# A graph layer with a Winograd-style convolution: the filter transform moved from VectorE to TensorE products

## The chip, the cores and the metric

The kernel runs on one core of one Trainium2 chip. The metric is the device time of one execution in microseconds. Engines are named as in the profile: PE is the matrix engine (PEld its weight loads), DVE the vector engine, ACT the scalar engine, POOL the GpSimd engine, SP the engine that issues most DMAs. Every engine executes its own instructions in the order in which the program lists them; a DMA is issued by SP, ACT or POOL and stands in that engine's order too.

## The reference

The input is x of 64 graphs with 256 nodes and 256 channels, and a 0/1 adjacency of 64 x 256 x 256. All is float32. After a layer norm and a rectifier (h), each graph goes through this layer, whose result is added to x:

```python
xc = jnp.transpose(x, (0, 2, 1))
h = jax.nn.relu(_bn(_conv1d(xc, conv1_w, 0), ...))           # 256 -> 256, one tap
h = _bn(_conv1d(h, conv2_w, 8), ...)                         # 256 -> 256, 17 taps along the nodes
x_conv = jnp.transpose(jax.nn.relu(h + xc), (0, 2, 1))
s = x @ w_se.T + b_se                                        # 3 numbers a node
A = jnp.exp(-dist(s)) * mask
x_nmp = A @ jax.nn.relu(x @ w_msg.T + b_msg)
gi = concat([x_conv, x_nmp]) @ w_ih.T + b_ih                 # then a GRU cell with
gh = x @ w_hh.T + b_hh                                       # gates r, z, n
```

The convolution with 17 taps (conv2) is the heavy part. It is computed in a transformed domain: along the nodes the signal is cut into pieces of 16, and a product of two polynomials is found from their values at 15 complex and 2 real points, arranged as 16 "bins": bins 0 to 14 are the complex points (roots of unity of several orders) and need three real products each, and bin 15 holds the two points 1 and -1 with one product each. So 15 x 3 + 2 = 47 matrices of 256 x 256 are needed from the filter. They are the filter's values at those points: the real part, and two combinations of real and imaginary part. The filter has 256 x 256 channel pairs with 17 taps each.

## The kernel before

**Units.** Two graphs form a pair (G = 2), handled as a tile of 512 columns (W); four pairs form a batch (PB = 4), and there are 8 batches (NB). conv2 works on a batch at a time, the other parts on a pair.

**The start.** The program first loads x for two pairs (SP), the taps of conv2 for the first 128 input channels (ACT, 17 DMAs), weights, and on POOL the small vectors (`vec`, line 375) and the adjacency. Lines 427 to 462 then transform the filter. Input channels lie on partitions. For each half of them (k = 0, 1) ACT copies the taps (line 433), DVE runs the same odd and even transforms that are used for the data (class `Fft`, `odd` at line 67 and `even` at line 97; their instructions have lines 55, 58 and 61), and `put` (line 425) stores each result from SP to `filt` in DRAM. `filt` is laid out by bin, then partition, kind of product, half and output channel, so that one bin is a block of 768 KB, 6 KB for each partition. The same buffers U, V, PT, Sv, T serve the filter here and the data later. Then come w_ih and w_hh (loaded by ACT), the batch norm vectors of conv2, and the sums of biases (`b_rz` at line 471, on DVE).

**Preparation of a pair.** `norm` (line 512) takes statistics of x on DVE, a power on POOL (line 526) and scales on DVE (line 530). `transpose_h` (line 534) transposes on PE, rectifies on ACT into HT, and issues the load of x two pairs ahead. `conv1` (line 548) does the one-tap convolution on PE and writes h1 from ACT (line 555). `split` (line 560) forms the sums and differences of h1 in U and V on DVE (lines 569 and 570). Before the first batch the four pairs are prepared one after the other (lines 779 to 783). Later preparations are spread between the gates of the batch before.

**The data's transform.** `forward` (line 771) queues the odd and even transforms of the batch on a list. The class `Pace` decides at each DVE instruction of the main order how many list entries to emit before it: it keeps estimated clocks of PE and DVE and emits entries as long as DVE is estimated to have time. `pace.flush(mark)` emits the rest up to a mark. `products` needs the odd part.

**The batch.** `products(b, m)` (line 596) does the bins 2m and 2m + 1 on PE, with weights from three rotating tiles WB. `load_bin` (line 575) loads bin n from `filt` on SP; the load of a bin waits until the tile's former bin has been used. Between the products stand `embed` (line 642), `message` (line 652), `affinity` (line 666), `transpose_a`, `aggregate`; after them the back transform, the residual and the `gates` (line 704). All PE products carry line 500 in the profile, all transposes line 504, since two helpers record them. A float32 product appears as two MATMUL records. PSUM has five tiles "acc" and three tiles "aux" of 512 columns. `load_y` (line 353) loads x again for the final addition, from POOL, the first two before the first preparation.

Of the kernel before, what the change touches and what calls it, by code (L numbers as in the profile page):

```python
# [3 lines left out]

# [34 lines left out]
class Fft:  # L39
# [221 lines left out]


class Mark:
    left = False
# [6 lines left out]
def kernel(  # L271
# [26 lines left out]
    nc = tc.nc  # L298
# [18 lines left out]
    const = ctx.enter_context(tc.tile_pool(name="const", bufs=1))  # L317
    work = ctx.enter_context(tc.tile_pool(name="work", bufs=1))
    psum = ctx.enter_context(tc.tile_pool(name="psum", bufs=1, space=bass.MemoryType.PSUM))
    dram = ctx.enter_context(tc.tile_pool(name="dram", bufs=1, space=bass.MemoryType.DRAM))  # L320
# [32 lines left out]
    def load_y(i):  # L353
        Y[i] = work.tile([P, G * MC, D], FP, name="y", bufs=2)
        load_rows(Y[i], x, i, nc.gpsimd)
# [6 lines left out]
    SL = GB * DC * L * NW  # L362
    Ut, Vt, Yvt = (const.tile([P, SL], FP, name=n) for n in ("U", "V", "Yv"))
    PTt, Svt, Tt = (const.tile([P, SL // 2], FP, name=n) for n in ("PT", "Sv", "T"))
# [27 lines left out]

    def load_taps(k):
        V = Slots(Vt, 1, L // 2, D)
        taps = c2_wT[k * P:(k + 1) * P]
        for c in range(2):
            for s in range(L // 2):
                t = L - (2 * (s - 4) + c) if s >= 4 else L - (8 + 2 * s + c)
                nc.scalar.dma_start(out=V(c, s)[:, 0, 0, :], in_=taps[:, t, :])
        w0 = work.tile([P, W], FP, name="tr")  # L400
        nc.scalar.dma_start(out=w0[:, :D], in_=taps[:, 0, :])
        return w0

    w0 = load_taps(0)
    w_c1 = const.tile([P, DC, D], FP)
    nc.sync.dma_start(out=w_c1, in_=c1_wT.rearrange("(k p) o -> p k o", p=P))
    w_se = const.tile([P, DC, KD], FP)
    nc.vector.memset(w_se, 0.0)
# [5 lines left out]
    s1, h1_shift = fold_bn(bn1, "bn1")  # L414
    w_msg = const.tile([P, DC, D], FP)
# [4 lines left out]


    filt = dram.tile([BINS, P, 3, DC, D], FP, name="filt")

    def put(bins, kind, k, t):
        nc.sync.dma_start(out=filt[bins:bins + t.shape[1], :, kind, k, :].rearrange("n p o -> p n o"), in_=t)

    for k in range(DC):
        if k > 0:
            w0 = load_taps(k)
        U, V = (Slots(t, 1, L // 2, D) for t in (Ut, Vt))  # L430
        PT, Sv, T = (Slots(t, 1, L // 4, D) for t in (PTt, Svt, Tt))
        for c in range(2):
            nc.scalar.copy(U(c, 0, 8), V(c, 0, 8))
        e0 = w0[:, :D].rearrange("p (a n e) -> p a n e", a=1, n=1)
        nc.vector.tensor_add(U(0, 4), V(0, 4), e0)
        nc.vector.tensor_sub(V(0, 4), V(0, 4), e0)
        for _, step in fft.odd(V, T, Sv):
            step()
        for c in range(2):
            put(c * 4, 0, k, V(c, 4, 4)[:, 0])  # L440
            put(c * 4, 2, k, Sv(c, 0, 4)[:, 0])
        nc.vector.tensor_sub(V(None, 0, 4), V(None, 0, 4), V(None, 4, 4))
        for c in range(2):
            put(c * 4, 1, k, V(c, 0, 4)[:, 0])
        for _, step in fft.even(U, PT, T):
            step()
        for c in range(2):
            put(8 + c * 2, 0, k, U(c, 0, 2)[:, 0])
            put(8 + c * 2, 2, k, U(c, 4, 2)[:, 0])
            put(12 + c, 0, k, PT(c, 2)[:, 0])  # L450
            put(12 + c, 2, k, U(c, 6)[:, 0])
        put(14, 0, k, PT(0, 1)[:, 0])
        put(14, 2, k, U(0, 7)[:, 0])
        put(15, 0, k, U(1, 7)[:, 0])
        put(15, 1, k, PT(1, 0)[:, 0])
        nc.vector.tensor_sub(U(None, 2, 2), U(None, 2, 2), U(None, 0, 2))
        nc.vector.tensor_sub(PT(None, 3), PT(None, 3), PT(None, 2))
        nc.vector.tensor_sub(PT(1, 1), PT(1, 1), PT(0, 1))
        for c in range(2):
            put(8 + c * 2, 1, k, U(c, 2, 2)[:, 0])  # L460
            put(12 + c, 1, k, PT(c, 3)[:, 0])
        put(14, 1, k, PT(1, 1)[:, 0])

    w_ih = const.tile([P, 2 * DC, 3 * D], FP)
    nc.scalar.dma_start(out=w_ih, in_=ih_wT.rearrange("(k p) o -> p k o", p=P))
    w_hh = const.tile([P, DC, 3 * D], FP)
    nc.scalar.dma_start(out=w_hh, in_=hh_wT.rearrange("(k p) o -> p k o", p=P))
    s2, h2_shift = fold_bn(bn2, "bn2", 1.0 / L)
# [17 lines left out]

    U, V, Yv = (Slots(t, GB * DC, L // 2, NW) for t in (Ut, Vt, Yvt))
    PT, Sv, T = (Slots(t, GB * DC, L // 4, NW) for t in (PTt, Svt, Tt))
# [5 lines left out]
    def acc():  # L494
        return psum.tile([P, W], FP, name="acc", bufs=5)
# [3 lines left out]
    def mm(p, w, v, columns, **kw):  # L499
        nc.tensor.matmul(p, w, v, **kw)  # L500
        pace.tensor(columns)
# [69 lines left out]


    WB = {}

    def load_bin(b, n):
        b, n = b + n // BINS, n % BINS
        if b < NB:
            WB[b, n] = work.tile([P, 3, DC, D], FP, name="wb", bufs=3)
            kinds = 3 if n < BINS - 1 else 2
            nc.sync.dma_start(out=WB[b, n][:, :kinds], in_=filt[n, :, :kinds])  # L580

# [14 lines left out]
    def products(b, m):  # L596
        load_bin(b, 2 * m + 2)
        p = [acc() for _ in range(3)]
        for n in range(2):
            for kind, v in enumerate(operands(2 * m + n)):  # L600
                if v is None:
                    continue
                for o in range(DC):
                    for k in range(DC):
                        mm(p[kind][:, (n * DC + o) * P:(n * DC + o + 1) * P],
                           WB[b, 2 * m + n][:, kind, k, o * P:(o + 1) * P],
                           v[:, k::DC, 0, :], P, start=(k == 0), stop=(k == DC - 1))
# [73 lines left out]
    def transpose_a(i):  # L681
        AT[i] = work.tile([P, G, MC, N], FP, name="aT")
        for g in range(G):
            q = aux()
            for c in range(MC):
                for r in range(MC):
                    transpose(q[:, c * N + r * P:c * N + (r + 1) * P], E[i][:, g, r, c * P:(c + 1) * P])
            nc.scalar.copy(AT[i][:, g].rearrange("p c n -> p (c n)"), q)  # L688

    def aggregate(i):  # L690
        XNM[i] = work.tile([P, DC, W], FP, name="xnm", bufs=2)
# [12 lines left out]
    def gates(i, dc, wait=None):  # L704
# [10 lines left out]
        product(ghn, h, n, True, True)  # L715
        gn = work.tile([P, W], FP, name="gn", bufs=2)
        nc.scalar.activation(gn, ghn, AF.Identity, bias=b_hh[:, 2 * DC + dc:2 * DC + dc + 1])
# [6 lines left out]
        product(pr, xc, r, False, True)  # L724
        tr = work.tile([P, W], FP, name="tr")
        nc.scalar.activation(tr, pr, AF.Tanh, bias=b_rz[:, dc:dc + 1], scale=0.5)  # L726
# [4 lines left out]
        nc.vector.scalar_tensor_tensor(gn, gn, 0.5, pn, op0=ALU.mult, op1=ALU.add)  # L731
        nn = work.tile([P, W], FP, name="nn", bufs=2)
        nc.scalar.activation(nn, gn, AF.Tanh, bias=b_ih[:, 2 * DC + dc:2 * DC + dc + 1])
        product(pz, xc, z, False, True)
        tz = work.tile([P, W], FP, name="tz")
# [3 lines left out]
        d = OT[i, dc] = work.tile([P, W], FP, name="d", bufs=3)  # L739
        nc.vector.tensor_sub(d, HT[i][:, dc, :], nn)  # L740
# [30 lines left out]
    def forward():  # L771
        pace.add(fft.odd(V, T, Sv), odd)
        pace.add(fft.even(U, PT, T), even)

    load_bin(0, 0)
    load_bin(0, 1)
    load_y(0)
    load_y(1)
    for j in range(PB):
        norm(j)  # L780
        transpose_h(j)
        conv1(j)
        split(j)
    forward()
    for b in range(NB):
# [120 lines left out]
```

## Time and profile before

| what | value |
|---|---|
| time, median of 3 runs | 2196.8 us (2194.21 to 2197.34) |
| profiled execution, its time | 2198.26 us |
| its span on the core | 2196.5 us |
| busy: PE, DVE, ACT, POOL | 1904.0, 1497.1, 623.5, 170.3 us |
| mean granted PE clock | 0.969 |
| DMA | 186.95 MB, mean 85 GB/s |

The profile is one execution, taken by the hardware profiler. Busy times are sums over an engine's instructions. In the rows of the time line, the number in front is the start in microseconds from the start of the span, the second the length of the row, then engine, line, operation, result and sources, and in brackets how long the engine stood idle before it and what ended the wait. "SPq" and the like are the DMA issues of an engine. In the busy tenths, each digit is a slice of 55 us. A share of the DMA engines of 1.00 means that all 16 are busy.

### The profile page before, as it was taken

Reading aid. Unit: us, or ns where it says so; the run is one execution under the profiler, and the core shown is the slowest. Engines: PE = TensorE matmul, PEld = TensorE weight load, DVE = VectorE, ACT = ScalarE, POOL = GpSimd, SP = SyncE. Lnnn points to the kernel's source line nnn. Section 1 sums busy time; section 2 is a strip of 40 time slices with the busy share of each in tenths; the row PEclk is TensorE's granted clock in tenths of the full one; section 3 lists DMA queues with packets and bytes.
Section 4 is the critical chain, followed back from the end, with each engine's and each line's share of the span. In section 5 each row is a group of like instructions: output and inputs, shape, how many; then the busy total and the mean of one; then the engine's idle time right before and its main releaser. Section 6 shows DMA issues by size and latency. Waiting matters only on the chain.

```text
span 2196.5 us, 20806 instructions
## 1 busy us (share of the span) xinstructions
PE 1904.0 (87%) x7744; PEld 1189.0 (54%) x7744; DVE 1497.1 (68%) x2737; ACT 623.5 (28%) x997; POOL 170.3 (8%) x255
## 2 busy tenths in 40 slices
PE   0023989999899989999899989999899989999897
PEld 0012944568444954568444854568445864468453
DVE  5866993678738784588738695587738785597622
ACT  0011243224232243224322243223322243222321
POOL 2010000010000000100000000100010000100000
PEclk9996999999999999999999999999999999999999
DMA  4551611245012620235012520326012530225011
GB/s 128 177 152 33 200 50 31 62 126 161 11 42 60 202 67 27 65 110 169 19 39 63 185 84 20 72 77 202 19 39 53 184 95 24 48 63 178 10 29 29
DMA packets 74453, 186.95 MB, mean 85 GB/s; under 512 B 19792, under 2 KB 36688, under 8 KB 74352
## 3 DMA queue, kind: packets, MB, share of 16 engines
q1 hardware_dynamic: 40448, 128.20, 17.8%
q0 software_dynamic: 28208, 50.60, 10.5%
q10 hardware_dynamic: 5696, 6.82, 1.0%
q8 instruction: 61, 1.00, 0.2%
q14 instruction: 40, 0.33, 0.0%
HBM read 156.39 MB, written 29.10 MB: 84 GB/s over the span
## 4 chain that ended last, share of the span: by engine, by line
PE 74%; DVE 14%; DMA 3%; ACT 2%; issue 2%; POOL 1%; POOLq 0%; DVEq 0%; ACTq 0%
PE acc L500 56%; PE aux L500 15%; PE aux L504 3%; DMA wb<-filt 3%; DVE V L55 2%; DVE V L58 2%; DVE T L61 1%; DVE T L58 1%; DVE Yv L61 1%; DVE V L61 1%; DVE Yv L638 1%; DVE e L677 1%; ACT Yv L639 1%; DVE T L55 1%; POOL rstd L526 0%
## 5 line engine op out<-in xcount | busy, mean ns | idle before, releaser
L500 PE MATMUL acc<-Yv,w_ih 128*128 128x512 f32 x768 | 357.4, 617 | 46.8 <-ACT Yv L639 46.8
L500 PE MATMUL acc<-hT,w_hh 128*128 128x512 f32 x768 | 350.6, 592 | 0.0
L500 PE MATMUL acc<-xnm,w_ih 128*128 128x512 f32 x768 | 350.4, 592 | 0.0
L500 PEld LDWEIGHTS acc<-Yv,w_ih 128*128 128x128 f32 x768 | 151.6, 199 | 243.4 <-issue 185.8
L500 PEld LDWEIGHTS acc<-xnm,w_ih 128*128 128x128 f32 x768 | 145.9, 190 | 183.7 <-issue 183.7
L500 PEld LDWEIGHTS acc<-hT,w_hh 128*128 128x128 f32 x768 | 144.1, 190 | 161.6 <-issue 156.4
L726 ACT ACTIVATE tr<-acc,b_rz 128x512 f32<-128x512 f32 x64 | 44.0, 687 | 553.6 <-PE acc L500 553.6
L504 PE MATMUL aux<-ident,x 128*128 128x128 f32 x256 | 40.3, 299 | 182.5 <-DVE x L530 161.3
L728 DVE SCALAR_TENSOR_TENSOR gn<-tr,gn 128x512 f32<-128x512 f32 x64 | 44.2, 691 | 209.3 <-ACT tr L726 209.3
L55 DVE SCALAR_TENSOR_TENSOR V<-T,V 128x256 f32<-128x256 f32 (+2 forms) x280 | 149.8, 609 | 0.5
L569 DVE TENSOR_TENSOR V<-h 128x512 f32<-128x512 f32 x64 | 44.0, 688 | 145.9 <-ACT h L555 145.9
L504 PEld LDWEIGHTS aux<-ident,x 128*128 128x128 f32 x256 | 32.0, 150 | 196.8 <-DVE x L530 163.8
L500 PE MATMUL acc<-V,wb 128*128 128x128 f32 x1024 | 128.9, 281 | 0.0
L500 PE MATMUL aux<-w_msg,hT 128*128 128x256 f32 x512 | 116.5, 380 | 12.9 <-ACT rd L649 12.9
L500 PE MATMUL aux<-aT,msg 128*128 128x256 f32 x512 | 126.0, 403 | 0.6 <-ACT aT L688 0.6
L500 PEld LDWEIGHTS acc<-V,wb 128*128 128x128 f32 x1024 | 124.0, 198 | 0.0
L500 PEld LDWEIGHTS acc<-U,wb 128*128 128x128 f32 x1024 | 120.0, 192 | 5.1 <-issue 2.5
L500 PE MATMUL acc<-U,wb 128*128 128x128 f32 x1024 | 122.1, 275 | 0.0
L500 PE MATMUL acc<-hT,w_c 128*128 128x512 f32 x256 | 119.3, 610 | 0.0
L500 PEld LDWEIGHTS aux<-w_msg,hT 128*128 128x128 f32 x512 | 96.1, 190 | 35.2 <-ACT rd L649 14.6
L500 PEld LDWEIGHTS aux<-aT,msg 128*128 128x128 f32 x512 | 102.3, 204 | 19.5 <-issue 3.8
L500 PE MATMUL acc<-Sv,wb 128*128 128x128 f32 x512 | 71.4, 285 | 37.8 <-DVE Sv L58 25.2
(134 smaller groups left out, 2640.1 us busy)
## 6 DMA issues: line engine op xcount, KB each, us to landing
wb<-filt SPq DMA_DIRECT2D x120, 768.0 KB
x<-in_x_dram SPq DMA_DIRECT2D x64, 256.0 KB
adj<-in_adj_dram POOLq DMA_DIRECT2D x64, 256.0 KB, 6.1
y<-in_x_dram POOLq DMA_DIRECT2D x64, 256.0 KB, 5.5
out_dram<-y POOLq DMA_DIRECT2D x64, 256.0 KB, 5.2
V<-in_c_wT_dram ACTq DMA_DIRECT2D x32, 128.0 KB
filt<-V SPq DMA_DIRECT2D x8, 512.0 KB
wb<-filt SPq DMA_DIRECT2D x8, 512.0 KB
```

The source lines that it names most:

```text
L55: return self.step(out, lambda: self.v.scalar_tensor_tensor(out, x, s, y, op0=ALU.mult, op1=ALU.add))
L58: return self.step(out, lambda: self.v.tensor_add(out, x, y))
L61: return self.step(out, lambda: self.v.tensor_sub(out, x, y))
L500: nc.tensor.matmul(p, w, v, **kw)
L504: nc.tensor.transpose(p, v, ident)
L569: nc.vector.tensor_sub(V(None, s, 4)[:, A], a, bb)
L638: nc.vector.scalar_tensor_tensor(v, v, s2[:, o:o + 1], HT[i][:, o, :], op0=ALU.mult, op1=ALU.add)
L639: nc.scalar.activation(v, v, AF.Relu, bias=h2_shift[:, o:o + 1])
L677: nc.vector.tensor_mul(e, e, ADJ[i][:, g * MC + c].rearrange("p (b h c) -> p c h b", c=MC, b=NW))
L726: nc.scalar.activation(tr, pr, AF.Tanh, bias=b_rz[:, dc:dc + 1], scale=0.5)
L728: nc.vector.scalar_tensor_tensor(gn, tr, 1.0, gn, op0=ALU.add, op1=ALU.mult)
```

## The change

Values of a polynomial with 17 coefficients at given points are a product with a constant matrix. The change forms that matrix (`filter_points`) for three groups of bins, 0 to 5, 6 to 11 and 12 to 15, with 18, 18 and 11 columns (kinds), and does the product on PE. Seven input channels with 17 taps each are laid on 119 partitions; the constant matrix is block-diagonal, 119 x 126 (or 119 x 77), so one product of 256 columns gives 7 channels x 18 kinds (or 11) on partitions, with the 256 output channels along the free dimension. Each half of 128 channels makes 18 such groups; the 2 + 2 channels left over form one more tile of 68 rows. A step `filters(m, j)` takes two groups: two products into one "acc" tile, one ACT copy into a staging tile ("fo", six of them), one store from SP. Three groups of bins x 19 steps are 57 steps. The first 48 stand in the preparation loop, twelve after each pair's `split`; nine stand after `forward`.

What else is moved:

- `norm(0)` stands before the loop, and `norm(j + 1)` between `transpose_h(j)` and `conv1(j)`.
- `filt` is three DRAM tiles (one for each group of bins), each by half, partition, kind, output channel. `load_bin` therefore fetches, for each partition, two pieces of up to 3 KB instead of one of up to 6 KB, and WB's inner order is half, kind.
- The first two `load_bin`, then w_ih and w_hh (now on SP), stand after the second pair's steps. The two `load_y` stand after all steps.
- The small vectors (`vec`) are loaded by SP instead of POOL, the weights of conv1 by ACT instead of SP, and the zeroing of w_se is on POOL instead of DVE.
- The taps, the constant matrices and the staging tiles live in a pool "stage" that is closed after the steps; its memory is used again by a pool "late" that holds Yv, y and the tiles of the gates.

```diff
+def filter_points(bins, taps):
+    cols = []
+    for n in bins:
+        z = [(ROOTS[n] if n < 15 else 1.0) ** (taps - 1 - t) for t in range(taps)]
+        if n < 15:
+            cols += [[v.real for v in z], [v.imag - v.real for v in z], [v.real + v.imag for v in z]]
+        else:
+            cols += [[1.0] * taps, [(-1.0) ** (taps - 1 - t) for t in range(taps)]]
+    return np.array(cols, np.float64).T
...
-        nc.gpsimd.dma_start(out=t, in_=src.rearrange("(k p) -> p k", p=P))
+        nc.sync.dma_start(out=t, in_=src.rearrange("(k p) -> p k", p=P))
...
-    def load_taps(k):
-        V = Slots(Vt, 1, L // 2, D)
...
+    KG = P // TAPS
+    NG = P // KG
+    REST = P - NG * KG
+    taps = stage.tile([KG * TAPS, DC * NG + 1, D], FP, name="taps")
+
+    def load_taps(dc, a, b, eng):
+        eng.dma_start(out=taps[:, dc * NG + a:dc * NG + b, :],
+                      in_=c2_wT[dc * P + a * KG:dc * P + b * KG].rearrange("(g k) t o -> (k t) g o", k=KG))
+
     w_c1 = const.tile([P, DC, D], FP)
-    nc.sync.dma_start(out=w_c1, in_=c1_wT.rearrange("(k p) o -> p k o", p=P))
+    nc.scalar.dma_start(out=w_c1, in_=c1_wT.rearrange("(k p) o -> p k o", p=P))
+    s1, h1_shift = fold_bn(bn1, "bn1")
+    PASSES = [range(0, 6), range(6, 12), range(12, 16)]
+    points = []
+    for n, bins in enumerate(PASSES):
+        f = filter_points(bins, TAPS)
+        m = np.zeros((KG, TAPS, KG, f.shape[1]), np.float32)
+        for k in range(KG):
+            m[k, :, k] = f
+        t = stage.tile([KG * TAPS, KG * f.shape[1]], FP, name=f"points{n}")
+        nc.scalar.dma_start(out=t, in_=nc.inline_tensor(m.reshape(KG * TAPS, -1), name=f"points{n}").ap())
+        points.append(t)
+    for dc in range(DC):
+        for h in range(2):
+            load_taps(dc, h * NG // 2, (h + 1) * NG // 2, nc.scalar if dc else nc.sync)
+        nc.sync.dma_start(out=taps[dc * REST * TAPS:(dc + 1) * REST * TAPS, DC * NG, :],
+                          in_=c2_wT[dc * P + NG * KG:(dc + 1) * P].rearrange("k t o -> (k t) o"))
...
-    for k in range(DC):
-        if k > 0:
-            w0 = load_taps(k)
...
-        for _, step in fft.odd(V, T, Sv):
-            step()
...
+    filt = [dram.tile([DC, P, t.shape[1] // KG, D], FP, name=f"filt{n}") for n, t in enumerate(points)]
+
+    def filters(m, j):
+        kinds = filt[m].shape[2]
+        groups = range(2 * j, min(2 * j + 2, DC * NG + 1))
+        size = REST * DC if groups[0] == DC * NG else KG
+        p = acc()
+        for n, g in enumerate(groups):
+            mm(p[:size * kinds, n * D:(n + 1) * D], points[m][:size * TAPS, :size * kinds],
+               taps[:size * TAPS, g, :], D, start=True, stop=True)
+        t = stage.tile([P, 2, D], FP, name="fo", bufs=6)
+        nc.scalar.copy(t[:size * kinds, :len(groups)].rearrange("p n o -> p (n o)"),
+                       p[:size * kinds, :len(groups) * D])
+        if size == KG:
+            dc, g = divmod(groups[0], NG)
+            nc.sync.dma_start(out=filt[m][dc, g * KG:(g + 2) * KG].rearrange("(g k) t o -> (k t) g o", k=KG),
+                              in_=t[:size * kinds])
...
-            WB[b, n] = work.tile([P, 3, DC, D], FP, name="wb", bufs=3)
...
-            nc.sync.dma_start(out=WB[b, n][:, :kinds], in_=filt[n, :, :kinds])
+            WB[b, n] = work.tile([P, DC, 3, D], FP, name="wb", bufs=3)
+            kinds, m = 3 if n < BINS - 1 else 2, n // len(PASSES[0])
+            first = 3 * (n - PASSES[m][0])
+            nc.sync.dma_start(out=WB[b, n][:, :, :kinds, :].rearrange("p k t o -> p k (t o)"),
+                              in_=filt[m][:, :, first:first + kinds, :].rearrange("k p t o -> p k (t o)"))
...
-    load_bin(0, 0)
-    load_bin(0, 1)
+    steps = [(m, j) for m in range(len(PASSES)) for j in range(NG + 1)]
+    norm(0)
+    for j in range(PB):
+        transpose_h(j)
+        norm(j + 1) if j + 1 < PB else None
+        conv1(j)
+        split(j)
+        for m, n in steps[j * 12:(j + 1) * 12]:
+            filters(m, n)
+        if j == 1:
+            load_bin(0, 0)
+            load_bin(0, 1)
+            nc.sync.dma_start(out=w_ih, in_=ih_wT.rearrange("(k p) o -> p k o", p=P))
+            nc.sync.dma_start(out=w_hh, in_=hh_wT.rearrange("(k p) o -> p k o", p=P))
+    forward()
+    for m, n in steps[PB * 12:]:
+        filters(m, n)
+    stage_ctx.close()
+    late = ctx.enter_context(tc.tile_pool(name="late", bufs=1, reuse_waits="tile"))
+    Yvt = late.tile([P, SL], FP, name="Yv")
+    Yv = Slots(Yvt, GB * DC, L // 2, NW)
     load_y(0)
     load_y(1)
-    for j in range(PB):
-        norm(j)
-        transpose_h(j)
-        conv1(j)
-        split(j)
-    forward()
```

More of the change, by code (lines that the diff above doesn't have):

```diff
@@ L318 @@
     work = ctx.enter_context(tc.tile_pool(name="work", bufs=1))
+    stage_ctx = ExitStack()
+    stage = stage_ctx.enter_context(tc.tile_pool(name="stage", bufs=1))
     psum = ctx.enter_context(tc.tile_pool(name="psum", bufs=1, space=bass.MemoryType.PSUM))
@@ L353, in load_y @@
     def load_y(i):
-        Y[i] = work.tile([P, G * MC, D], FP, name="y", bufs=2)
+        Y[i] = late.tile([P, G * MC, D], FP, name="y", bufs=2)
         load_rows(Y[i], x, i, nc.gpsimd)
@@ L362 @@
     SL = GB * DC * L * NW
-    Ut, Vt, Yvt = (const.tile([P, SL], FP, name=n) for n in ("U", "V", "Yv"))
+    Ut, Vt = (const.tile([P, SL], FP, name=n) for n in ("U", "V"))
     PTt, Svt, Tt = (const.tile([P, SL // 2], FP, name=n) for n in ("PT", "Sv", "T"))
@@ L389, in fold_bn @@
         return scale, shift
-    def load_taps(k):
-        V = Slots(Vt, 1, L // 2, D)
[L395 to L404, printed above, removed]
-    w_c1 = const.tile([P, DC, D], FP)
-    nc.sync.dma_start(out=w_c1, in_=c1_wT.rearrange("(k p) o -> p k o", p=P))
+    KG = P // TAPS
[5 more added lines that the diff above has]
+                      in_=c2_wT[dc * P + a * KG:dc * P + b * KG].rearrange("(g k) t o -> (k t) g o", k=KG))
+    w_c1 = const.tile([P, DC, D], FP)
+    nc.scalar.dma_start(out=w_c1, in_=c1_wT.rearrange("(k p) o -> p k o", p=P))
[15 more added lines that the diff above has]
+                          in_=c2_wT[dc * P + NG * KG:(dc + 1) * P].rearrange("k t o -> (k t) o"))
     w_se = const.tile([P, DC, KD], FP)
-    nc.vector.memset(w_se, 0.0)
+    nc.gpsimd.memset(w_se, 0.0)
     for r in (0, 32, 64):
@@ L485 @@
     nc.gpsimd.memset(h1, 0.0)
[L487 removed]
+    U, V = (Slots(t, GB * DC, L // 2, NW) for t in (Ut, Vt))
     PT, Sv, T = (Slots(t, GB * DC, L // 4, NW) for t in (PTt, Svt, Tt))
@@ L570, in split @@
             nc.vector.tensor_add(U(None, s, 4)[:, A], a, bb)
+    filt = [dram.tile([DC, P, t.shape[1] // KG, D], FP, name=f"filt{n}") for n, t in enumerate(points)]
[14 more added lines that the diff above has]
+                              in_=t[:size * kinds])
+        else:
+            for dc in range(DC):
+                nc.sync.dma_start(out=filt[m][dc, NG * KG:].rearrange("k t o -> (k t) o"),
+                                  in_=t[dc * REST * kinds:(dc + 1) * REST * kinds, 0, :])
     WB = {}
@@ L681, in transpose_a @@
     def transpose_a(i):
-        AT[i] = work.tile([P, G, MC, N], FP, name="aT")
+        AT[i] = late.tile([P, G, MC, N], FP, name="aT")
         for g in range(G):
@@ L690, in aggregate @@
     def aggregate(i):
-        XNM[i] = work.tile([P, DC, W], FP, name="xnm", bufs=2)
+        XNM[i] = late.tile([P, DC, W], FP, name="xnm", bufs=2)
         for dc in range(DC):
@@ L715, in gates @@
         product(ghn, h, n, True, True)
-        gn = work.tile([P, W], FP, name="gn", bufs=2)
+        gn = late.tile([P, W], FP, name="gn", bufs=2)
         nc.scalar.activation(gn, ghn, AF.Identity, bias=b_hh[:, 2 * DC + dc:2 * DC + dc + 1])
@@ L724, in gates @@
         product(pr, xc, r, False, True)
-        tr = work.tile([P, W], FP, name="tr")
+        tr = late.tile([P, W], FP, name="tr")
         nc.scalar.activation(tr, pr, AF.Tanh, bias=b_rz[:, dc:dc + 1], scale=0.5)
@@ L731, in gates @@
         nc.vector.scalar_tensor_tensor(gn, gn, 0.5, pn, op0=ALU.mult, op1=ALU.add)
-        nn = work.tile([P, W], FP, name="nn", bufs=2)
+        nn = late.tile([P, W], FP, name="nn", bufs=2)
         nc.scalar.activation(nn, gn, AF.Tanh, bias=b_ih[:, 2 * DC + dc:2 * DC + dc + 1])
         product(pz, xc, z, False, True)
-        tz = work.tile([P, W], FP, name="tz")
+        tz = late.tile([P, W], FP, name="tz")
         nc.scalar.activation(tz, pz, AF.Tanh, bias=b_rz[:, DC + dc:DC + dc + 1], scale=0.5)
         pace.vector(W, pace.dve + ACT)
-        d = OT[i, dc] = work.tile([P, W], FP, name="d", bufs=3)
+        d = OT[i, dc] = late.tile([P, W], FP, name="d", bufs=3)
         nc.vector.tensor_sub(d, HT[i][:, dc, :], nn)
```

45 lines of the change are left out of this document (6 added, 39 removed).

## The prediction

> **What bounds the kernel now.** I read the busy tenths of the page first, then the busy time stage by stage, then the time line of the start, and the steady part last. The page's 40 slices of 55 us:
>
> ```profile
> span 2196.5 us, 20806 instructions
> PE   0023989999899989999899989999899989999897
> DVE  5866993678738784588738695587738785597622
> ```
>
> PE is nearly full from the fifth slice to the end and idle in the first two; no later slice looks like the start. Busy time by stage (stretch, length, then busy time and count of PE, PEld, DVE, ACT, POOL, granted clock, DMA share, GB/s):
>
> ```profile
> 0.00:23.00 23.00, 0.00 (x0) 0.00 (x0) 1.12 (x6) 4.11 (x3) 13.07 (x25) 1.00 0.78 192
> 23.00:131.00 108.00, 0.00 (x0) 0.00 (x0) 99.67 (x157) 4.66 (x3) 0.00 (x0) 1.00 0.41 136
> 131.00:137.00 6.00, 0.00 (x0) 0.00 (x0) 1.80 (x10) 0.00 (x0) 5.64 (x9) 1.00 0.95 294
> 137.00:192.00 55.00, 30.72 (x78) 15.77 (x79) 22.53 (x69) 12.81 (x19) 6.26 (x8) 0.81 0.41 111
> 192.00:219.00 27.00, 1.77 (x9) 1.24 (x7) 25.93 (x44) 2.09 (x4) 0.00 (x0) 0.57 0.00 0
> 717.10:965.80 248.70, 236.12 (x970) 147.53 (x970) 174.18 (x322) 76.59 (x124) 19.20 (x28) 0.98 0.29 84
> ```
>
> From 23 to 131 us DVE alone works: the filter transform, 99.67 of 108 us, with PE at zero. Then come the four preparations (137 to 192), then the data's own transform on DVE (192 to 219). A later batch of four is bound by PE, 236 of 249 us, and the change leaves its arithmetic alone. So I cost the first 219 us, and ask of the rest only whether the bin loads stay hidden. The time line (start, length, engine, line, what, and the idle time before with its releaser):
>
> ```profile
> 130.62 0.42 DVE L458 TENSOR_TENSOR PT<-PT 128x256 f32<-128x256 f32 x1
> ...
> 136.28 0.16 DVE L471 TENSOR_TENSOR b_rz<-b_ih,b_hh 128x4 f32<-128x4 f32 x1 [3.26 <-DMA b_hh<-in_hh_b_dram]
> ...
> 136.81 1.38 DVE L519 BATCH_NORM_STATS2 st<-x 128x6 f32<-128x256 f32 x4
> ...
> 147.55 0.78 ACT L555 ACTIVATE h<-acc,bn_shift,bn_scale 128x512 f32<-128x512 f32 x1 [0.88 <-PE acc L500]
> ...
> 167.99 2.30 PE L504 MATMUL aux<-ident,x 128*128 128x128 f32 x8 [6.87 <-DVE x L530]
> ...
> 181.65 2.30 PE L504 MATMUL aux<-ident,x 128*128 128x128 f32 x8 [6.87 <-DVE x L530]
> ...
> 188.54 0.78 ACT L555 ACTIVATE h<-acc,bn_shift,bn_scale 128x512 f32<-128x512 f32 x1 [0.99 <-PE acc L500]
> ...
> 191.17 0.69 DVE L570 TENSOR_TENSOR U<-h 128x512 f32<-128x512 f32 x1
> ...
> 194.32 1.22 DVE L61 TENSOR_TENSOR T<-V 128x1024 f32<-128x1024 f32 x1
> ...
> 218.84 2.07 PE L500 MATMUL acc<-Sv,wb 128*128 128x128 f32 x8 [25.23 <-DVE Sv L58]
> ```
>
> The first bin product starts at 218.84. What moves that start moves the end by as much.
>
> **Removed.** All DVE and ACT work of lines 433 to 458, the 108 us above, and 46 puts of 12.3 MB. As many bytes are put back: 57 steps of two products, one ACT copy, one put on SP. Sizes of single transfers, by the view of DMA issues:
>
> ```profile
> wb<-filt SPq DMA_DIRECT2D x120, 768.0 KB
> x<-in_x_dram SPq DMA_DIRECT2D x64, 256.0 KB
> ...
> V<-in_c_wT_dram ACTq DMA_DIRECT2D x32, 128.0 KB
> ...
> w_ih<-in_ih_wT_dram ACTq DMA_DIRECT2D x1, 1536.0 KB
> ...
> w_hh<-in_hh_wT_dram ACTq DMA_DIRECT2D x1, 768.0 KB
> ```
>
> **Term 1, the start of the first norm.** DVE is in order, and ahead of norm(0) stands b_rz, which needs b_hh (the 3.26 us wait above). That load moves from POOL to SP, behind both halves of the first taps. SP also holds back a load when too many are under way:
>
> ```profile
> SPq L406 <- DMA x<-in_x_dram: 4.8, 1, 4.8
> SPq L416 <- DMA V<-in_c_wT_dram: 3.0, 1, 3.0
> ```
>
> Neither load needs what it waited for; I read this as a limited number of transfers in flight, so b_hh goes out about when the last taps land. How fast do taps land in tiles of 119 rows? One-microsecond windows where an x load runs alone (outer dimension 8 in DRAM), where bin loads of 128 rows run, and where puts of 128 rows in 1 KB pieces run:
>
> ```profile
> 159.00:160.00 1.00, 1.00 (x3) 0.39 (x3) 0.00 (x0) 0.56 (x1) 0.00 (x0) 1.00 0.49 188
> 188.00:189.00 1.00, 1.00 (x4) 0.28 (x2) 0.00 (x0) 0.46 (x1) 0.00 (x0) 1.00 1.05 293
> 109.00:113.00 4.00, 0.00 (x0) 0.00 (x0) 3.97 (x3) 0.00 (x0) 0.00 (x0) 1.00 1.03 339
> ```
>
> A share of 0.49 is 8 of 16 engines for outer dimension 8, and 128 rows fill all. [...] One engine moves 339/16 = 21.2 GB/s in 1 KB pieces, so 4.46 MB of taps take 4.46/(7 x 0.0212) = 30.1 us; bounds 13.1 (all 16) and 46 (half of the first window's 192 GB/s). With first issue 0.7, x ahead on the same engines 1.05 MB/188 = 5.6, other weights and adjacency 1.2 MB/339 = 3.5, the wait for b_hh 3.3 and the 0.5 us from b_rz to norm: T0 = 43.7, say 44 (27 to 60). What else moves lies ahead of T0 and is needed later: bn1's loads (POOL to SP) and w_c (SP to ACT) at conv1(0), the three constant matrices (ACT, 0.2 MB) at the first step, the memset of w_se (DVE to POOL).
>
> **Term 2, first preparation.** From norm(0) to the end of conv1's products is 136.81 to 147.5 in the rows: 10.7 us, clock still rising.
>
> **Term 3, three loops.** A preparation now repeats every 13.66 us (181.65 - 167.99), mostly a chain through DVE and POOL. The new order issues norm(j+1) ahead of conv1(j), so that part lies under the filter steps. Full-clock rows, the put's issue on SP, and an ACT copy of the same size:
>
> ```profile
> 280.32 1.04 PE L504 MATMUL aux<-ident,x 128*128 128x128 f32 x8
> ...
> 282.94 3.62 PE L500 MATMUL aux<-w_msg,hT 128*128 128x256 f32 x16
> ...
> 286.39 3.60 PE L500 MATMUL acc<-hT,w_c 128*128 128x512 f32 x8
> ...
> 71.32 0.46 SPq L425 DMA_DIRECT2D filt<-PT  x1
> ...
> 224.83 0.59 ACT L612 COPY p<-acc 128x512 f32<-128x512 f32 x1 [29.76 <-PE acc L500]
> ```
>
> A product of 256 columns is two of the 16 records: 0.45 us; a step is 0.905. A loop on PE is transposes 1.04, about 1.4 until ACT gives both halves of hT, conv1 3.60, twelve steps 10.86: 16.9 us. [...] The put is unshown; bounds are 0.76 (16 engines) and 1.52 (half). [...] Three loops: 50.7. After the second, SP takes two bin loads, which wait for the first filter tile's puts (the 19th of 24, long issued), and w_ih and w_hh: 3.9 MB, 11.6 us at 339. The puts of loop three queue behind them; six staging and five PSUM tiles absorb all but some 2 us. x loads stand behind twelve puts on SP, yet each is needed a whole loop later: nothing. At the granted clock of 0.81 that the preparations have now, the PE part would be 4 us more a loop (16.9/0.81 less 16.9), +12; I take full clock, because the steps keep PE busy. conv1(3) ends at T0 + 63.4.
>
> **Term 4, the data transform.** From the end of conv1 to the last split is 188.5 to 191.9, 3.4 us; the transform with the wait for its last sum is 194.32 to 218.84, 24.5; the message additions queued among it add 1.5. PE meanwhile has 21 steps (19.0), embed and message (5.5): done at T0 + 88, before DVE's T0 + 92.8. Yv and the y loads now wait until the staging memory is free, which is when the last steps are through, T0 + 82 and a put's return; behind the y loads POOL has batch 1's norm, some 40 us later: nothing, and without that cover the put's return of a few us.
>
> **Term 5, bin loads.** They fetch the same bytes as 256 pieces of 3 KB instead of 128 of 6 KB. One in sixteen is late now:
>
> ```profile
> PE acc L500 <- DMA wb<-filt: 12.5, 7, 2.4
> 477.85 8.06 DMA wb<-filt
> ```
>
> About 1.8 us a batch behind a load of 8.06 us that shares the engines with adjacency and output. I take +2 us over the kernel: puts in 1 KB pieces still reach 339 GB/s, so smaller pieces alone cost little (bounds 0 and 14).
>
> [...]
>
> **Sum.** First bin product at 44 + 92.8 = 136.8, 82.0 earlier; less 2: 80 off the profiled execution's 2198.3 (its span plus 1.8), 2118. The median shown is 1.5 lower: **2117**.
>
> **The rivals.**
> A. Puts at half rate, 1.52 each. conv1(3) then waits for put 29: T0 + 12 + 28 x 1.52 + 11.6 + three x loads 8.4 = 74.6 instead of 59.8: **2132**. For it: nothing shows 126 rows; against: 128 rows fill 16 engines.
> B. Taps on all 16 engines, the lower bound of term 1: 17 us earlier, **2100**. Against: the 0.49.
> [...]
> D. The loop doesn't overlap: 13.66 + 10.86 = 24.5 a loop, +23, **2140**. It would need norm(j+1) stuck behind a filter step; neither DVE nor POOL holds one.
> E, the other side. The puts of 126 rows go out on very few engines. ACT's embed stands behind copy 56, which needs put 50 landed; the start reaches 218.84 when 51 puts take 218.84 - 44 - 12 - 11.6 - 11 - 5.5 = 135 us, 2.6 each, under 99 GB/s or five engines. On two engines 6.1 us for each full put: some **2340**. Against: the x load's 188.
>
> **Chances.** Forecast 0.50 (its own range 2107 to 2126), A 0.17, B 0.11, C 0.13, D 0.05, E 0.04. I take 2098 to 2142, which leaves out E and the tails. Under 0.2% (4 us) a measurement can't be told from no change: faster 0.95, same 0.01, slower 0.04.
>
> **What would show it.** First norm near 44 us with a DMA share near 0.45 while the taps load (all 16: B); preparations 17 us apart with PE busy in between and ACT not waiting for puts (A if it does); first bin product near 137; batches still 248.7 apart and the fifth bin's wait near 2 us (C if 4). I am wrong if the start lies beyond 165 or the batches lengthen by over 2 us.

## The result, and the profile after

The changed kernel takes 2121.56 us (median of 4 runs, 2119.11 to 2122.57) against 2197.07 for the kernel before in the same comparison: a ratio of 0.9655 [0.9639, 0.9672], 75.5 us faster. Predicted were 2117, range 2098 to 2142. The profiled execution took 2119.11 us, where the prediction's sum, before it was set against the median, gave 2118.3. The page's span and busy tenths, slices of 53 us:

```profile
span 2117.3 us, 21204 instructions
PE   0889899998999899998999989998999989999897
DVE  1379846796387845968367873879549784688532
```

PE is idle in one slice, where it was idle in two and mostly idle in two more. The stages (stretch, length, busy time and count of PE, PEld, DVE, ACT, POOL, granted clock, DMA share, GB/s):

```profile
30.00:34.00 4.00, 0.00 (x0) 0.00 (x0) 0.00 (x0) 0.00 (x0) 0.00 (x0) 1.00 0.48 167
59.00:112.50 53.50, 46.37 (x191) 34.94 (x190) 13.78 (x38) 28.45 (x48) 2.01 (x2) 0.94 0.81 269
112.50:143.00 30.50, 22.93 (x101) 15.19 (x100) 28.38 (x48) 16.29 (x28) 2.42 (x4) 0.94 0.62 176
391.00:640.00 249.00, 236.10 (x970) 147.45 (x970) 174.22 (x323) 76.81 (x124) 19.23 (x28) 0.98 0.28 84
```

No stretch with DVE alone is left. The three loops of preparation and steps (59 to 112.5) run on PE, 46 of 53.5 us; the rest to the first bin product runs on DVE, 28 of 30.5. A later batch looks as it did, 236 of 249 us on PE. The time line (start, length, engine, line, what, and the idle time before with its releaser; the matmul helper is line 491 now, norm 510 to 521, the filter copies 577):

```profile
22.07 13.63 SPq L442 DMA_DIRECT2D taps<-in_c_wT_dram  x2
...
40.59 1.17 SPq L399 DMA_DIRECT2D bn_v<-in_bn_v_dram  x1
...
44.64 0.55 SPq L399 DMA_DIRECT2D b_hh<-in_hh_b_dram  x1
...
45.79 0.17 DVE L406 TENSOR_SCALAR bn_scale<-bn_v 128x2 f32<-128x2 f32 x1 [28.37 <-DMA bn_v<-in_bn_v_dram]
...
47.33 0.40 DVE L462 TENSOR_TENSOR b_rz<-b_ih,b_hh 128x4 f32<-128x4 f32 x1
...
47.93 1.40 DVE L510 BATCH_NORM_STATS2 st<-x 128x6 f32<-128x256 f32 x4
...
59.00 10.53 PE L491 MATMUL acc<-taps,points 119*126 119x256 f32 x48
...
70.74 3.70 PE L491 MATMUL acc<-hT,w_c 128*128 128x512 f32 x8 [0.34 <-ACT hT L533]
...
74.28 10.10 PE L491 MATMUL acc<-taps,points 119*126 119x256 f32 x46
...
89.14 9.66 PE L491 MATMUL acc<-taps,points 119*126 119x256 f32 x44
...
104.14 2.02 ACT L577 COPY fo<-acc 126x512 f32<-126x512 f32 x3 [9.00 <-DMA filt<-fo]
104.78 2.07 PE L491 MATMUL acc<-taps,points 119*126 119x256 f32 x4 [5.99 <-ACT fo L577]
...
112.56 17.56 PE L491 MATMUL acc<-taps,points 119*126 119x256 f32 x80
...
115.98 1.22 DVE L64 TENSOR_TENSOR T<-V 128x1024 f32<-128x1024 f32 x1
...
143.01 2.05 PE L491 MATMUL acc<-Sv,wb 128*128 128x128 f32 x8 [7.58 <-issue]
```

The first bin product starts at 143.01 instead of 218.84, 75.8 us earlier, and the whole gain is there: from it to the end of the span are 1974.3 us, before 1977.7, and executions of one kernel differ by as much. The gain has two parts of opposite sign. The first norm starts at 47.93 instead of 136.81, 88.9 earlier; from there to the first bin product are 95.1 us instead of 82.0, 13.1 more, since that stretch now holds the filter steps: 36 of the 57 ahead of the last preparation's end, the rest beside the transform.

Two things stand out against the forecast. The loads of the small vectors are issued late (40.59, 44.64), behind two loads that held SP for 13.63 us, 12.95 of them the first. And the third loop is 23.4 us long (112.56 - 89.14), with ACT waiting 9.00 us for a put; the first two took 15.3 and 14.9. The chain of waits names what stood ahead of those puts (start, length, what):

```profile
88.45 12.28 DMA w_hh<-in_hh_wT_dram
...
100.80 6.99 DMA filt<-fo
```

The bin loads, in pieces of half the size, are waited for as little as before (12.5 us in 7 waits then; waited for, total, times, longest):

```profile
PE acc L491 <- DMA wb<-filt: 13.9, 7, 2.8
```

### The profile page after: what moved, and what is told of

It is laid out like the page before. It is cut to its first block, busy times and chain, and to the rows that moved or that the text cites. A ratio compares the mean times of both kernels' runs of the same rounds, so it can differ in the third digit from the quotient of the medians.

```text
span 2117.3 us, 21204 instructions
## 1 busy us (share of the span) xinstructions
PE 1944.6 (92%) x7966; PEld 1221.2 (58%) x7966; DVE 1396.6 (66%) x2580; ACT 648.0 (31%) x1050; POOL 162.8 (8%) x246
## 4 chain that ended last, share of the span: by engine, by line
PE 76%; DVE 13%; DMA 5%; ACT 3%; issue 2%; SPq 1%; POOL 1%; ACTq 0%; POOLq 0%; DVEq 0%
PE acc L491 58%; PE aux L491 15%; PE aux L495 3%; DMA wb<-filt 3%; DVE V L61 2%; DVE Yv L64 1%; DVE T L64 1%; DVE Yv L656 1%; DVE V L64 1%; DVE T L61 1%; DVE V L58 1%; DMA taps<-in_c_wT_dram 1%; DVE e L695 1%; SPq L442 1%; ACT Yv L657 1%
## 5 line engine op out<-in xcount | busy, mean ns | idle before, releaser
L491 PE MATMUL aux<-w_msg,hT 128*128 128x256 f32 x512 | 116.5, 380 | 12.9 <-ACT rd L667 12.9
L58 DVE SCALAR_TENSOR_TENSOR V<-T,V 128x256 f32<-128x256 f32 (+2 forms) x224 | 120.0, 609 | 0.3
L491 PEld LDWEIGHTS aux<-aT,msg 128*128 128x128 f32 x512 | 101.2, 202 | 19.3 <-issue 3.8
L491 PE MATMUL acc<-Sv,wb 128*128 128x128 f32 x512 | 70.2, 281 | 21.5 <-DMA wb<-filt 13.9
L772 POOL DMA_DIRECT2D out_dram<-y x64 | 39.1, 615 | 642.3 <-DVE y L771 618.8
```

Of the source, the lines that this page charges most:

```text
L58: return self.step(out, lambda: self.v.scalar_tensor_tensor(out, x, s, y, op0=ALU.mult, op1=ALU.add))
L772: nc.gpsimd.dma_start(out=rows(out, G * i + g), in_=row_tile(Y[i], g))
```

## The experiments

The theory after the result: the start of the first norm is set by the taps, whose loads of 119 rows leave about half of the 16 engines idle (share 0.48), and by vector loads queued behind them; the third loop's stall comes from the transfers of w_ih and w_hh ahead of the puts; the gain is the DVE work taken away. The rivals: that the order of the preparations alone makes much of the gain, that the steps' interleaving does, that the bin layout costs or gains something, and that the taps' time doesn't depend on the number of rows. Each run is compared with the kernel before on its own chip (2198.2 to 2198.6).

### Taps on more engines

```diff
-        eng.dma_start(out=taps[:, dc * NG + a:dc * NG + b, :],
-                      in_=c2_wT[dc * P + a * KG:dc * P + b * KG].rearrange("(g k) t o -> (k t) g o", k=KG))
+        src = c2_wT[dc * P + a * KG:dc * P + b * KG].rearrange("(g k) t o -> (k t) g o", k=KG)
+        for lo, hi in ((0, 112), (112, KG * TAPS)):
+            eng.dma_start(out=taps[lo:hi, dc * NG + a:dc * NG + b, :], in_=src[lo:hi])
```

> The changed kernel with each load of taps cut in two by rows, 112 rows (16 x 7) and 7 rows, same bytes to the same places. [...] Rival (memory, or the number of transfers in flight, sets the pace): share and landing stay, no change within 3 us.

Measured: 2113.10 us, ratio 0.9617 [0.9600, 0.9635]. A stage while the taps load, and rows of the time line:

```profile
20.00:30.00 10.00, 0.00 (x0) 0.00 (x0) 0.00 (x0) 0.00 (x0) 5.47 (x9) 1.00 1.04 218
```

```profile
20.44 4.45 SPq L443 DMA_DIRECT2D taps<-in_c_wT_dram  x2
...
40.14 1.40 DVE L511 BATCH_NORM_STATS2 st<-x 128x6 f32<-128x256 f32 x4
...
137.87 2.04 PE L492 MATMUL acc<-Sv,wb 128*128 128x128 f32 x8 [7.58 <-issue]
```

The share doubles, from 0.48 to 1.04: in 112 rows the taps keep all 16 engines busy, in 119 about half of them. But the rate rises only from 167 to 218 GB/s, so the load gets 1.3 times faster, not 2.2 times as the share does: the first norm comes 7.8 earlier, and the first bin product 5.1. Rival B of the prediction had its condition met here and gave 8 us, not 17.

### The same in smaller loads

Why do sixteen busy engines move so little? One reading: a tile of 18 groups reads 1 KB pieces that lie far apart. Here each group is loaded by itself.

```diff
-        for lo, hi in ((0, 112), (112, KG * TAPS)):
-            eng.dma_start(out=taps[lo:hi, dc * NG + a:dc * NG + b, :], in_=src[lo:hi])
+        for g in range(a, b):
+            eng.dma_start(out=taps[:112, dc * NG + g, :], in_=src[:112, g - a])
+        eng.dma_start(out=taps[112:, dc * NG + a:dc * NG + b, :], in_=src[112:])
```

> e_taps16 with the 112-row loads of taps issued one for each group of seven channels (36 transfers of 112 KB, each one block of DRAM) instead of nine groups in one transfer; the same 1 KB pieces in another order. In e_taps16 all engines were busy and yet moved only 218 GB/s, and the last tap landed at 35 us, not at 28. Theory A (pieces 119 KB apart in memory read slowly): the taps land near 28 us, first bin product some 6 us earlier than e_taps16's 138.0. Theory B (reads of 1 KB pieces are that slow in any order, or what is left over, 7 and 34 rows on few engines, ends last): no change within 2 us, 2113 us.

Measured: 2117.72 us, ratio 0.9628 [0.9611, 0.9645]. The same stage:

```profile
20.00:30.00 10.00, 0.00 (x0) 0.00 (x0) 0.00 (x0) 1.28 (x1) 1.11 (x2) 1.00 1.05 223
```

The rate stays (223 against 218), so the order of the pieces is not the cause. The first bin product of this execution, at 133.02, comes 4.9 us earlier than in the run before (137.87), but only 1.2 of that lies ahead of the first norm (38.97 against 40.14), and the profiled execution is the fastest of four by 4.4 us; the intervals of the two runs overlap, so no gain is shown. What limits the rate stays open. The size of the pieces alone isn't it: puts of the same 1 KB pieces reach 339 GB/s in the profile before, and there the second half of the taps, loaded by ACT in 128 rows of 1 KB pieces, moved 254 GB/s:

```profile
57.00:63.00 6.00, 0.00 (x0) 0.00 (x0) 6.00 (x12) 0.00 (x0) 0.00 (x0) 1.00 0.86 254
```

### Vector loads ahead of the taps

```diff
     s1, h1_shift = fold_bn(bn1, "bn1")
+    s2, h2_shift = fold_bn(bn2, "bn2", 1.0 / L)
+    b_ih, b_hh = vec(ih_b, "b_ih"), vec(hh_b, "b_hh")
```

(and their former place, behind w_msg, is empty)

> The changed kernel with the ten small vector loads that DVE needs ahead of the first norm (those of bn2, b_ih, b_hh) moved ahead of the taps on SP, nothing else. Theory (the first norm at 47.9 us waits for b_hh, which stands behind the taps on SP; only the filter steps need the taps): the first norm starts between 20 and 30 us, the first pair is prepared while the taps land, the first steps run from about 37 us and go on at 44 when the last taps of the first half are there, and the first bin product comes 13 to 18 us earlier: about 2106 us against 2121.6. Rival (the taps themselves set the start, since PE's steps stand between the preparations): the gain is only the first preparation's conv1, under 5 us.

Measured: 2109.58 us, ratio 0.9599 [0.9581, 0.9616]. The time line:

```profile
21.93 16.27 SPq L444 DMA_DIRECT2D taps<-in_c_wT_dram  x1
...
29.04 1.38 DVE L510 BATCH_NORM_STATS2 st<-x 128x6 f32<-128x256 f32 x4
...
40.12 4.05 PE L491 MATMUL acc<-taps,points 119*126 119x256 f32 x18
44.99 5.88 PE L491 MATMUL acc<-taps,points 119*126 119x256 f32 x26 [0.81 <-DMA taps<-in_c_wT_dram]
...
59.84 10.10 PE L491 MATMUL acc<-taps,points 119*126 119x256 f32 x46
...
129.66 2.05 PE L491 MATMUL acc<-Sv,wb 128*128 128x128 f32 x8 [7.58 <-issue]
```

The first norm starts 18.9 us earlier, with the taps as slow as they were. So what held the first norm was not that it needs the taps, but six small loads issued behind them (four for bn2, b_ih and b_hh; the expectation says ten). The taps themselves are needed only at the first step, and are a little late there now (0.81 us). The first loop, which meets the taps' last transfers, takes 19.7 us (59.84 - 40.12) instead of 15.3; of the 18.9 us 13.3 arrive at the first bin product.

### The GRU weights behind the last step

```diff
-            nc.sync.dma_start(out=w_ih, ...)
-            nc.sync.dma_start(out=w_hh, ...)
 ...
+    nc.sync.dma_start(out=w_ih, ...)
+    nc.sync.dma_start(out=w_hh, ...)
     stage_ctx.close()
```

> The changed kernel with the loads of w_ih and w_hh moved on SP from behind the second pair's steps to behind the last step. Theory (the third loop's 23.4 us against 15 of the others is the puts standing behind 2.4 MB of weights and two bins in SP's queue): the third loop falls to 16 or 17 us, the first bin product comes 6 to 8 us earlier, 2114 us against 2121.6. Rival (the six staging tiles return too slowly in themselves): the third loop stays above 20 us, no change within 2 us.

Measured: 2116.55 us, ratio 0.9634 [0.9616, 0.9651]. The intervals of this and of the changed kernel overlap, so the time alone doesn't tell them apart; the time line does:

```profile
73.12 10.10 PE L491 MATMUL acc<-taps,points 119*126 119x256 f32 x46
...
88.05 10.53 PE L491 MATMUL acc<-taps,points 119*126 119x256 f32 x48
...
96.60 0.58 ACT L577 COPY fo<-acc 126x512 f32<-126x512 f32 x1 [2.54 <-DMA filt<-fo]
97.38 0.58 ACT L577 COPY fo<-acc 126x512 f32<-126x512 f32 x1 [0.19 <-DMA filt<-fo]
...
106.83 17.56 PE L491 MATMUL acc<-taps,points 119*126 119x256 f32 x80
...
137.29 2.04 PE L491 MATMUL acc<-Sv,wb 128*128 128x128 f32 x8 [7.58 <-issue]
```

The third loop shrinks from 23.4 to 18.8 us, not to the 16 or 17 expected, ACT's wait from 9.00 to 2.54, and the first bin product comes 5.7 earlier, 4.6 of it by the third loop; the first steps of this execution start 1.2 earlier already. The weights are more than half of the stall. That the 3.9 us that are left against the second loop's 14.9 come from the two bin loads and x loads ahead of the puts is likely, not shown. Where the puts set ACT's pace, a copy comes about every 0.77 us (0.78 from 96.60 to 97.38).

### The order of the preparations without the change

In the kernel before, with its filter transform on DVE:

```diff
+    norm(0)
     for j in range(PB):
-        norm(j)
         transpose_h(j)
+        norm(j + 1) if j + 1 < PB else None
         conv1(j)
```

> The kernel before, with only the order of the norms changed as the change does it: norm(0) ahead of the loop, norm(j + 1) between transpose_h(j) and conv1(j). The filter stays on DVE. Theory (most of the gain is DVE's 108 us of filter work that is gone): a loop falls from 13.7 to about 9 us, the first bin product comes 12 to 15 us earlier, 2184 us against 2197. Rival (the order of the preparation is what gains): over 40 us.

Measured: 2177.13 us, ratio 0.9905 [0.9884, 0.9925]. The time line:

```profile
138.63 2.30 PE L504 MATMUL aux<-ident,x 128*128 128x128 f32 x8 [138.63 <-DVE x L530]
...
146.41 1.04 PE L504 MATMUL aux<-ident,x 128*128 128x128 f32 x8
...
154.53 2.30 PE L504 MATMUL aux<-ident,x 128*128 128x128 f32 x8 [2.89 <-DVE x L530]
...
161.30 1.74 PE L504 MATMUL aux<-ident,x 128*128 128x128 f32 x8
...
197.39 2.08 PE L500 MATMUL acc<-Sv,wb 128*128 128x128 f32 x8 [25.23 <-DVE Sv L58]
```

A preparation repeats every 7 to 8 us instead of 13.66, and the first bin product comes 21.4 earlier, more than the 12 to 15 expected; 2.1 of that lies ahead of the first norm (134.68 here), 19.3 behind it. So as much as a good quarter of the gain is to be had without the matrix form, by the one line that issues a norm ahead of the convolution before it. No run has the matrix form with the old order, so what the order is worth inside the changed kernel is not shown.

### All steps behind the preparations

With the GRU weights late, as above:

```diff
     for j in range(PB):
         ...
-        for m, n in steps[j * 12:(j + 1) * 12]:
-            filters(m, n)
     forward()
-    for m, n in steps[PB * 12:]:
+    for q, (m, n) in enumerate(steps):
         filters(m, n)
+        if q == 23:
+            load_bin(0, 0)
+            load_bin(0, 1)
```

> The changed kernel with all 57 steps behind the four preparations (and behind the queueing of the data's transform) instead of twelve between them, and w_ih and w_hh behind the steps as in e_late. Theory (PE's own work and DVE's transform are what fills the start, and the steps cover either the preparations or the transform, not both): a preparation loop takes about 7.5 us, as in e_order, 57 steps 50 us with the transform under them; the first bin product comes within 3 us of e_late's 137.6, time 2113 to 2119. Rival (standing between the preparations is what hides the steps): 10 us or more later than e_late.

Measured: 2120.55 us, ratio 0.9644 [0.9627, 0.9662]. The time line:

```profile
57.26 1.04 PE L495 MATMUL aux<-ident,x 128*128 128x128 f32 x8
64.23 1.73 PE L495 MATMUL aux<-ident,x 128*128 128x128 f32 x8 [1.75 <-DVE x L521]
71.00 1.73 PE L495 MATMUL aux<-ident,x 128*128 128x128 f32 x8 [1.09 <-DVE x L521]
76.52 29.95 PE L491 MATMUL acc<-taps,points 119*126 119x256 f32 x138
110.62 21.04 PE L491 MATMUL acc<-taps,points 119*126 119x256 f32 x84 [4.14 <-ACT fo L577]
...
136.82 1.05 PE L491 MATMUL acc<-Sv,wb 128*128 128x128 f32 x8
...
150.42 2.07 PE L491 MATMUL acc<-Sv,wb 128*128 128x128 f32 x8 [6.35 <-DMA wb<-filt]
```

The first bin product stands where it stood with the weights late (136.8 against 137.3). So the interleaving in itself is worth nothing at the first bin product. The steps take some 50 us of PE wherever they are: between the preparations they cover what DVE and POOL do for the norm, behind them they cover the transform, and the one cover costs the other. The median is 4.0 us above the kernel with the weights late and 1.5 above what was expected, but the intervals overlap; the trace has a reason for it: the weights go out after the last step, which comes later here, and the third bin load behind them is waited for 6.35 us (all of PE's waits for bins: 19.4 us against 13.7).

### Smaller bin pieces alone

The kernel before, with `filt` laid out by half, partition, bin, kind, so that a bin load fetches 256 pieces of 3 KB:

```diff
-    filt = dram.tile([BINS, P, 3, DC, D], FP, name="filt")
+    filt = dram.tile([DC, P, BINS, 3, D], FP, name="filt")
 ...
```

(the put, the bin load and the order inside WB follow the layout)

> The kernel before, with only the filter's layout in DRAM and the order inside a bin tile changed, so that each bin load is 256 pieces of 3 KB instead of 128 of 6 KB. The puts write the same 1 KB pieces to other places. Theory (same bytes, all engines, one bin in sixteen a little late): the wait for bins goes from 1.8 to about 2 us a batch, time within +3 us of 2197. [...]

Measured: 2198.43 us, ratio 1.000 [0.9991, 1.001]. PE's waits:

```profile
PE acc L500 <- DMA wb<-filt: 12.9, 7, 3.0
```

12.9 us in 7 waits against 12.5. The halved pieces cost nothing that shows; the interval leaves room for 2 us either way.

### The fixes together

Taps in 112 + 7 rows, all issued by ACT; the vector loads ahead; the loads of small weights and adjacency (POOL) and of w_msg (SP) behind norm(0); nine steps a loop, and the bin loads behind the third pair's steps. In the first version w_ih and w_hh go out behind the last step; in the second they are cut into six loads behind bin loads of the first batch:

```diff
         load_bin(b, 2 * m + 3)
+        if b == 0 and m < 6:
+            w, src, k = (w_ih, ih_wT, m) if m < 4 else (w_hh, hh_wT, m - 4)
+            nc.sync.dma_start(out=w[:, k, :], in_=src[k * P:(k + 1) * P])
```

> The changed kernel with what the runs point to put together: taps in 112 and 7 rows, all on ACT; the vectors ahead; POOL's weight loads and the adjacency behind the first norm; nine steps between the preparations instead of twelve, 30 after the last; the first two bin loads behind the third pair; w_ih and w_hh behind the last step. Theory: the first norm starts near 15 us, the last tap lands near 36, the four preparations run under the taps' landing and the first steps, and PE's 57 steps set the pace: first bin product between 97 and 108 us, time 2078 to 2090 us against 2121.6. Rival (with the taps on all engines the x loads of the third and fourth pair starve, and PE stands behind them): first bin product at 120 or later, 2100 us.

> e_best with w_ih and w_hh cut in six pieces of 384 KB, each on SP behind the second bin load of one of the first six product blocks of batch 0, instead of both behind the last step. Theory (e_best's batch 0 lasts 255.2 us against 248 because its third bin stands behind 2.4 MB of weights): the 6.2 us wait for that bin goes, batch 0 falls to 248 to 250 us, first bin product stays near 107.5, 2086 to 2089 us against 2092.5. Rival (batch 0 is longer because the last puts and the y loads share the engines): batch 0 stays above 253, no change.

Measured: 2092.54 us, ratio 0.9517 [0.9502, 0.9532], and 2083.20 us (2079.11 to 2085.90), ratio 0.9477 [0.9460, 0.9494]. The first is slower than its 2078 to 2090, the second faster than its 2086 to 2089. The time line of the first version:

```profile
20.89 1.40 DVE L496 BATCH_NORM_STATS2 st<-x 128x6 f32<-128x256 f32 x4
...
107.53 1.05 PE L477 MATMUL acc<-Sv,wb 128*128 128x128 f32 x8
...
120.92 2.08 PE L477 MATMUL acc<-Sv,wb 128*128 128x128 f32 x8 [6.15 <-DMA wb<-filt]
```

The first bin product comes 35.5 us earlier than in the changed kernel, but the time falls by 29: the third bin load stands behind the 2.36 MB of w_ih and w_hh, and PE waits 6.15 us for it. PE's waits for bins in the second version:

```profile
PE acc L477 <- DMA wb<-filt: 12.4, 8, 2.0
```

12.4 us in all instead of 20.3. The second version beats both kernels: 115 us faster than the one before and 38 us faster than the changed one. The parts of these two runs act together; only those tried above are known alone.

## Why the prediction was right

Its reading held: one number, the start of the first bin product, carries the change, and the batches behind it repeat every 249 us as before. The terms from the rows above, predicted and measured:

| term | predicted | measured | by |
|---|---|---|---|
| first norm, T0 | 44 | 47.9 | +3.9 |
| to the first steps | 10.7 | 11.1 (59.00 - 47.93) | +0.4 |
| three loops with the stall | 50.7 + 2 | 53.6 (112.56 - 59.00) | +0.9 |
| to the transform | 3.4 | 3.4 (115.98 - 112.56) | 0 |
| transform with messages | 26.0 | 27.0 (143.01 - 115.98) | +1.0 |
| first bin product | 136.8 | 143.0 | +6.2 |
| the rest of the span | 1977.7 + 2 | 1974.3 | -5.4 |

So the sum met the profiled execution to 1 us with help from errors that cancel: 6.2 us late at the first bin product, 5.4 us short behind it. The bin loads cost PE 1.4 us more of waiting instead of 2 (the upper bound of 14 was the author's estimate), and the rest came out 3.4 us shorter than before, which is no more than executions of one kernel differ by (2119.11 to 2122.57; the profiled one is the fastest). Against the median the forecast was 4.6 us short.

**Term 1.** The size was nearly right, the mechanism half. That b_hh goes out late, when the last taps land, is what the trace shows: SP waited 2.5 us for a tap transfer ahead of b_ih (44.23), and b_hh followed at 44.64. But the wait that ended last is not b_hh's: b_rz started without one (47.33), and DVE stood until 45.79 for bn_v, whose load had been issued at 40.59, behind SP's issue of 13.63 us. The prediction's sum holds transfers alone, up to 39.9 (0.7 + 5.6 + 3.5 + 30.1); its 21.2 GB/s an engine is close to what moved (167 GB/s at a share of 0.48, 21.7 for each busy engine), and that issue is not in it. The seven engines in it were the author's estimate; the traces give shares, and 0.48 is 7.7 of 16. That a limited number of transfers in flight is behind SP's waits was a reading too; the traces show the waits alone (4.8 and 3.0 us before, 2.5 us here). How much of the 3.9 us is issue and how much transfer was not separated. What was sized as a transfer was a queue: with the taps just as slow and the vectors ahead of them, the norm starts at 29.04.

**Term 2.** The clock, said to be still rising there, was granted in full: 1.00 from 137 to 142 us and from 142 to 147 in the profile before. What the traces show is the slower pace of the first products, 4.64 us for conv1's eight at 142.88 against 3.60 at 286.39, and 5.46 in the changed kernel, whose granted clock from 45 to 59 us was 1.00 too.

**Term 3.** The loop was sized too long and the stall too short. Twelve steps take 10.53 us (48 records), 0.88 each and not 0.905, and a loop 15 and not 16.9, above all since PE waits 0.34 us for hT and not 1.4; the error of some 5.6 us over three loops met a stall of 8.5 instead of 2 (23.4 less 14.9). That "six staging and five PSUM tiles absorb all but some 2 us" is the step that failed: at one copy every 0.88 us six staging tiles last 5.3 us, and the transfer of w_hh ended at 100.73, 12.28 us after its issue, with the puts behind it. The place was right, and moving the weights removed 4.6 of the 8.5 us. The granted clock in the loops was 0.94, near the full clock that I took and not the 0.81 of the old preparations.

**Term 4** and the order of the preparations held. The loops overlap as forecast (rival D falls), and the run with the order alone shows the same 7 to 8 us a preparation without any steps.

**Rivals.** A, puts at half rate: ACT's copies come about every 0.77 us where the puts set the pace, near the lower bound of 0.76 and not 1.52. C, bin loads that lose share: 13.9 us in 7 waits here, and a ratio of 1.000 when the smaller pieces are tried alone. E, puts on very few engines: the share of 0.81 over the loops excludes it. B needed all 16 engines, and with 119 rows the share was 0.48; with 112 rows it was 1.04, and the gain is 8 us and not the 17 it was priced at, since the rate of a busy engine falls from 21.7 to 13.1 GB/s (218 at a share of 1.04).

What the prediction doesn't say is what the parts are worth alone: in the kernel before, the new order of the preparations by itself gives 19 to 21 us, against 75.5 for the whole change, and another 38 lay in the fixes together: how, and in which order, the loads are issued, and how many steps stand in each loop.

## What to carry to other kernels

When the work of a start is moved, list every load that the first instruction waits for, by the queue that issues it and in order: moving six small loads ahead of the taps gained 12 us here, loading the taps in 112 rows, with all engines busy (share 1.04 instead of 0.48), 8. Bulk loads that are needed late go behind the small stores that the path needs now, and in pieces, or the next load that is needed soon waits for all of them (PE stood 6.15 us for a bin load behind 2.36 MB). And where a change mixes a new order with a new algorithm, run the order alone before the gain is put down to the algorithm.

## What was unexpected of the hardware

A DMA issue can hold its sequencer for long without a wait in the profile: of two loads of 34 rows, the first took SP 12.95 us to issue behind taps in 119 rows, and 16.27 us with the vectors ahead. Behind taps in 112 rows, both together took 4.45 us. Why the issue is so long was not tried.

Twice as many busy engines didn't double the rate: loads of 1 KB pieces moved 167 GB/s at a share of 0.48 and 218 to 223 at 1.04 and 1.05, with the pieces in either order. A busy share is not a rate, and what limits these loads stays open.
